# A two-layer cross-attention decoder on one core: earlier loads of rows and value weights, and later exponentials in one step

## Chip, core and metric

The kernel runs on one core of a Trainium2 chip. A core has five engines that run their own instruction queues: TensorE (PE in the profile; its weight loads are listed as PEld), VectorE (DVE), ScalarE (ACT), GpSimd (POOL) and SyncE (SP), which here only issues DMAs. ACT and POOL can issue DMAs too. The metric is the device time of one execution in microseconds (us). Before the change it is 2435.92 us, the median of three runs (2434.83 to 2436.45).

## The reference

Two batches of 512 rows of width 1024 (`x`) pass through four blocks, all in float32 unless noted. `ctx` has 1024 rows of width 1024 per batch.

```python
# layer 0
x = x + fake_quant(layernorm(x)) @ fake_quant(ctx)           # 8-bit grids: exact in bf16
x = x + h @ W.T + b + lora(h, softmax(mean(h) @ router))     # h = layernorm(x)
# layer 1
h = layernorm(x)
q = rope(h @ wq); k = rope(ctx @ wk); v = ctx @ wv           # 32 query heads, 8 key heads, width 128
a = softmax(q @ k.T / sqrt(128) + mask) @ v
x = x + a @ wo
x = x + layernorm(x) @ W_up.T + top-1 lora
```

Keys and values of layer 1 depend on `ctx` alone and not on `x`, so they can be computed first.

## The kernel before

**Seven products.** Every large float32 product is cut into 2 x 2 blocks and done with seven block products instead of eight (`seven`, L258, in the order 1, 2, 6, 7, 5, 4, 3; `seven_onto` for sums onto rows). Sums and differences of the operand blocks are made by VectorE: `left_steps` (L230; additions at L233, L236, L238, L241) for weights and `right_steps` (L244; L247, L250, L252, L255) for the context. A product accumulates in a PSUM bank; banks are shared by products 1 and 2, 7 and 4, 5 and 3. So product 2 must wait until ACT has copied product 1 out (L274), product 4 until VectorE has read product 7 (L281), and product 3 until VectorE has read product 5 (L283). Product 6 is read at L278, products 4 and 3 at L287 and L290. All of these matmuls go through `accumulate`, so their line is L345.

**Order of the stages.** TensorE's order is that of the program. The first stage is the keys of batch 0 (`keys`, L475): two quads of heads, each in two groups. Its loads stand at L1031 to L1070: key weights (pool `u4`, eight tiles of 4 KB per partition) and the four quarters of the transposed context (pool `u8`), on SP and ACT, then rope tables and small constants on SP. Each finished key block is turned by `rope` (L196; two ACT copies L204/L205, then VectorE L207, L210, L211) and stored by SP (L487). After the keys come the values of batch 0 (`values`), then keys and values of batch 1. Layer 0 (`layer_0`, `quantized_product`, L410) is woven between their products: for each batch eight row tiles of `ctx` are loaded (L414) and quantized by VectorE (L182, L185, L186), the four row tiles of `x` are normalized (`layernorm`: statistics L151 twice and L152 for each tile, square root on ACT L163, reciprocal L164, scaling L156) and quantized with the same three lines, then transposed (L424) and multiplied.

**What sets the order of the other engines.** A planner orders the instructions of each engine by when it expects their inputs, earlier lines of the program first. Inside `manual_schedule` blocks the named engines keep the program's order: VectorE and ACT in the first stage (L1088 to L1119), VectorE, ACT and POOL in the attention (L1287 on). Instructions from outside such a block may still be set between those of the block, where the planner expects a wait. Each pool has a fixed number of slots (`u8` 14, `u4` 17, `u2` 10, `small` 16). Slots are given in the program's order of first use, slots never used ahead of those given back; a tile's first writer waits for the slot's last user. SP and ACT issue DMAs in their own order, and an issue that waits holds up all behind it.

**The lines of this change.** The rows of batch 0 are loaded by `load_rows(0, nc.scalar)` (L1119), the last statement of the first stage's manual block, four DMAs of 512 KB on ACT. The first value weights are loaded by `raw_weights(wv, 0)` (L1144), four DMAs of 512 KB on SP, just before the second quad of keys is run and woven with layer 0; they are needed by the values' sums at L233 and following. 

**The attention's start.** `attention` (L851) runs one head per step n, from −2 on. In a step, the scores of head n+2 go to PSUM in four pairs (`scores`, L761; the two wide PSUM buffers), VectorE adds the mask and so frees each buffer (L777), and `tree` finds the maximum (L785 to L791), which is turned by TensorE into another wide buffer (L727) and reduced by VectorE (L729). For head n+1, `place_maximum` copies the maximum to a PSUM bank (L805) and `exponential` subtracts it (L809), takes the exponential on ACT (L812) and sums on POOL (L815 to L820). In steps −2 and −1 no head is ready for its products, and the last products of the queries fill TensorE instead: four of them in step −1 (L920), with the exponentials of head 0 set between them (L922 to L926). The ropes of these products are finished later, at `rotate` (L939).

Of the kernel before, what the change touches and what calls it, by code (L numbers as in the profile page):

```python
# [39 lines left out]
def decoder_kernel(  # L40
# [25 lines left out]
    nc = tc.nc  # L66
# [286 lines left out]

    def quad_weights(dram, q):

        return quad_sums(raw_weights(dram, q))

    def raw_weights(dram, q):
        raw = []
        for mh in range(2):  # L360
            for ch in range(2):
                w = u4([P, 4, 256])
                nc.sync.dma_start(w, dram[q, mh, ch])
                raw.append(w)
        return raw

    def quad_sums(raw):
        return left_sums(nc.vector, *raw, lambda: u4([P, 4, 256]))

    x = [None] * B  # L370
# [4 lines left out]
    def halves():  # L375
        return [u8([P, 2, D]) for _ in range(2)]
# [7 lines left out]
    def load_rows(b, queue):  # L384
        for t in range(NT):
            queue.dma_start(rows(b, t), x_in[b, ts(t, P), :])
# [464 lines left out]
    def attention(extra):  # L851

        total = B * NH
        heads, outs, kv = {}, {}, {}
        stretches = iter(())

        def rotate():  # L860
            for rotation in extra["later"]:
                next(rotation, None)
            extra["later"].clear()

        def begin(n):
            if n >= total:
                return
            gg = n // GRP
            if gg not in kv:
                b, g = gg // NKV, gg % NKV  # L870
                kT = u4([P, S2])
                nc.sync.dma_start(kT, kT_d[b][g])
                v = u4([P, NKT, DH])
                nc.sync.dma_start(v, v_d[b][g // 2][:, :, ts(g % 2, DH)])
                kv[gg] = kT, v
                outs[gg] = u8([P, GRP, S])
            heads[n] = Head(n, kv[gg], outs[gg][:, n % GRP, :])

        begin(0)
        for n in range(-2, total + GRP + 1):  # L880
            new, mid, old = heads.get(n + 2), heads.get(n + 1), heads.get(n)
            begin(n + 3)
            if new:
                for j in range(4):
                    new.scores(j)
            yield

            if n - 1 in heads:
                heads.pop(n - 1).normalize()
            if n == GRP - 1 or n == NH:  # L890
                fetch_rows(n // NH)

            if GRP <= n <= total and n % GRP == 0:
                oT = outs.pop(n // GRP - 1)
                sums = u8([P, 3, 2, 256])
                places = iter(range(3))
                o_ops = left_sums(
                    nc.gpsimd,
                    oT[:, 0:2, 0:256],
                    oT[:, 2:4, 0:256],  # L900
                    oT[:, 0:2, 256:S],
                    oT[:, 2:4, 256:S],
                    lambda: sums[:, next(places)],
                )
                following = n // GRP - 1, o_ops
            tree = new.tree() if new else iter(())
            k = (n - 1) % GRP
            if n > GRP and k == 0:
                gg, o_ops = following
                stretches = projection(gg // NKV, o_ops, dict(w_ops))  # L910
            for _ in range(3 + k % 2 if n > GRP else 0):
                next(stretches, None)
                next(tree, None)
            if n > GRP and gg + 1 < B * NKV:
                for i in {2: (1, 6, 2), 3: (7, 5, 4, 3)}.get(k, ()):
                    w_ops[i] = output_operand((gg + 1) % NKV, i)
            for i in range(extra.pop(n, 0)):
                for _ in range(2):
                    next(tree, None)
                next(extra["products"])  # L920

                if mid and not old and i == 1:  # L922
                    mid.place_maximum()
                    mid.exponential(0)
                if mid and not old and i == 2:
                    mid.exponential(1)  # L926
            if n == GRP:
                w_ops = {i: output_operand(0, i) for i in (1, 6, 2, 7, 5, 4, 3)}
            for _ in tree:
                pass  # L930
            yield

            if mid and old:
                mid.place_maximum()
            if old:
                old.turn_sum()
            elif new:
                new.turn_maximum()
            rotate()  # L939
            if old:  # L940
                old.attend(0)
                if mid:
                    mid.exponential(0)
                if new:
                    new.turn_maximum()
                if mid:
                    mid.exponential(1)
                old.den = from_row(old.den)
            if new:
                new.nmx = from_row(new.nmx)  # L950
            if old:
                old.attend(1)
            yield
# [114 lines left out]
    nc.sync.dma_start(eb_t, ebias.partition_broadcast(P))  # L1068
    nc.sync.dma_start(r0_t, r0T.rearrange("(c p) e -> p c e", p=P))
    nc.sync.dma_start(ga_t, gaT.rearrange("(c p) e -> p c e", p=P))  # L1070


    ctx_ops = [ctx_raw[0], ctx_raw[2]] + [None] * 5
    w = [wk_raw[q][0:2] + [None] * 5 for q in range(2)]
# [13 lines left out]
    with tc.manual_schedule(engines={mybir.EngineType.DVE, mybir.EngineType.Activation}):  # L1088
        rights = right_steps(nc.vector, *ctx_raw, lambda: u8([P, 4, HALF]))
        lefts = left_steps(nc.vector, *wk_raw[0], lambda: u4([P, 4, 256]))  # L1090
        advance(rights, 2)
        advance(lefts, 2)
        for c in range(4):
            for m in range(2):
                nc.tensor.matmul(
                    begun[m],
                    wk_raw[0][0][:, c, ts(m, P)],
                    ctx_raw[0][:, c, :],
                    start=(c == 0),
                    stop=(c == 3),  # L1100
                )
        for g in first[0]:
            next(g)
        next(first[0][0])
        next(rights)
        next(lefts)
        next(first[0][1])
        w[0][:] = next(lefts)
        ctx_ops[:] = next(rights)
        for _ in range(2):  # L1110
            for g in first[1]:
                next(g)
        lefts = left_steps(nc.vector, *wk_raw[1], lambda: u4([P, 4, 256]))
        for i, _ in enumerate(chain(*first[0])):
            if i in (4, 5, 6, 7):
                w[1][:] = next(lefts) or w[1]

        x[0] = halves()
        load_rows(0, nc.scalar)  # L1119

    for side in ("x1", "x2"):
        nc.vector.reciprocal(qp[f"{side}_inv"], qp[f"{side}_scale"])
    for c_t, side in ((c_x1, "x1"), (c_x2, "x2")):
# [5 lines left out]
    for b in range(B):  # L1129
        if b == 1:  # L1130
            for ch in range(2):
                ctx_raw[2 * ch + 1] = context_quarter(1, ch, 1, nc.scalar)
            w = quad_weights(wk, 0)
            ctx_ops = context_sums(ctx_raw)
        for i, stage in enumerate((keys, keys, values, values)):
            if (b, i) == (0, 0):
                continue
            if (b, i) == (0, 3):
                ctx_raw = [None] * 4
                for ch in range(2):  # L1140
                    ctx_raw[2 * ch] = context_quarter(1, ch, 0, nc.scalar)
            if (b, i) == (0, 1):
                main = chain(*first[1])
                raw = raw_weights(wv, 0)  # L1144
                weave(main, side, 2)
                w = quad_sums(raw)
            else:
                main = pair(*stage(b, i % 2, ctx_ops, w))
                weave(main, side, 2)
                if i < 3:  # L1150
                    w = quad_weights((wk, wv)[(i + 1) // 2], (i + 1) % 2)
            if i == 1 and b == 1:
                for _ in side:
                    pass
                ab_t = u8([P, 2, D])
                a_t, b_t = ab_t[:, 0].rearrange("p (c m) -> p c m", c=NC), ab_t[:, 1]
                nc.sync.dma_start(a_t, a0T.rearrange("(c p) m -> p c m", p=P))
                nc.gpsimd.dma_start(b_t, b0.partition_broadcast(P))  # L1158
                tT = [None] * B
                fetch_rows(0)  # L1160
                hs, steps = normed(0, u8, 2)
                side = chain(steps, routed(0, hs, a_t, b_t, tT))
# [30 lines left out]
    w = [quad_weights(wq, 0), quad_weights(wq, 1)]  # L1193
# [12 lines left out]
    for q in range(NH // 4):  # L1206
# [9 lines left out]
        if q < NH // 4 - 1:  # L1216
# [6 lines left out]
            if q > 0:  # L1223
                w = quad_weights(wq, q + 1)
# [207 lines left out]
```

## Time and profile before

| what | us |
|---|---|
| median of three runs | 2435.92 |
| profiled execution, whole | 2434.64 |
| its span, first to last instruction | 2432.8 |
| TensorE busy | 2407.8 |
| VectorE busy | 1842.8 |
| GpSimd busy | 1024.5 |
| ACT busy | 527.2 |
| rows of batch 0 issued (ACT, four) | 71.97 to 74.06 |
| value weights issued (SP, four) | 57.05 to 72.15 |
| last constant issued (SP) | 27.86 |

The profile is of one execution, so sums are made against 2434.64 and carried over to the median. A line of a timeline begins with the start and the duration in us; then come the engine, the line of the kernel, the operation, the tile written and the tiles read, their shapes and the number of merged instructions; the bracket holds the idle time just before and what ended it. In a table by stretches, the columns are the stretch's length, the busy time of TensorE, its weight loads, VectorE, ACT and POOL (with the number of instructions), the granted TensorE clock (1.00 is full), the busy share of the 16 DMA engines, and GB/s. TensorE's matmuls are pipelined, and their ends are modelled.

### The profile page before, as it was taken

How to read it: one execution, taken by the hardware profiler on the slowest of the kernel's cores; microseconds unless marked ns; L12 is line 12 of the kernel's file. 1: busy time of each engine (PE TensorE's matmuls, PEld its weight loads, DVE VectorE, ACT ScalarE, POOL GpSimd, SP SyncE). 2: the span in 40 equal slices, each digit the busy share in tenths (PEclk: the TensorE clock that was granted, in tenths of full speed). 3: DMA queues.
4: the chain of work that ended last, by engine and by line, in shares of the span. 5: the costliest groups of instructions: out<-in, count | busy, mean ns of one | idle time of the engine just before them, and what ended most of it. 6: DMA issues, size and time to landing. Idle time of an engine off the chain costs nothing.

```text
span 2432.8 us, 19529 instructions
## 1 busy us (share of the span) xinstructions
PE 2407.8 (99%) x6792; PEld 1195.1 (49%) x6792; DVE 1842.8 (76%) x1998; ACT 527.2 (22%) x623; POOL 1024.5 (42%) x543
## 2 busy tenths in 40 slices
PE   9999999999999999999999999999999999999999
PEld 4477458654444444444444444444444444444444
DVE  5849774345986556898888888888898988888753
ACT  1210221011222222322222222222223222222210
POOL 0000010210000002777676767667776767677531
PEclk9999999999999999999999999999999999999999
DMA  5437133013796221344223323442332243233501
GB/s 197 169 99 281 70 131 112 26 61 116 280 334 212 78 90 53 101 141 117 75 80 106 117 68 89 143 143 79 129 117 78 95 123 116 66 91 109 173 9 61
DMA packets 151506, 288.01 MB, mean 118 GB/s; under 512 B 32112, under 2 KB 49776, under 8 KB 149104
## 3 DMA queue, kind: packets, MB, share of 16 engines
q1 hardware_dynamic: 110880, 244.54, 30.6%
q10 hardware_dynamic: 40384, 41.70, 5.6%
q8 instruction: 54, 0.88, 0.1%
q0 software_dynamic: 144, 0.52, 0.1%
q14 instruction: 44, 0.36, 0.1%
HBM read 223.54 MB, written 63.18 MB: 118 GB/s over the span
## 4 chain that ended last, share of the span: by engine, by line
PE 55%; DVE 4%; issue 1%; POOL 0%; ACT 0%; POOLq 0%; DVEq 0%; ACTq 0%
PE b L345 20%; PE wide L763 16%; PE b L826 16%; PE wide L727 2%; DVE u L809 1%; DVE u L777 0%; DVE u L789 0%; DVE small L729 0%; DVE u L318 0%; DVE u L787 0%; PE b L967 0%; PE wide L192 0%; DVE u L791 0%; DVE u L785 0%; PE wide L1016 0%
## 5 line engine op out<-in xcount | busy, mean ns | idle before, releaser
L345 PE MATMUL b<-u,u 128*128 128x512 f32 (+1 forms) x3600 | 1384.5, 541 | 14.8 <-DVE u L283 4.2
L345 PEld LDWEIGHTS b<-u,u 128*128 128x128 f32 x3600 | 681.3, 191 | 684.0 <-issue 605.2
L826 PE MATMUL b<-u,u 128*128 128x512 f32 x1024 | 460.3, 592 | 0.0
L763 PE MATMUL wide<-u,u 128*128 128x512 f32 x1024 | 452.6, 593 | 2.6 <-DVE u L777 1.7
L815 POOL TENSOR_TENSOR u<-u 128x1024 f32<-128x1024 f32 x64 | 151.6, 2368 | 705.3 <-ACT u L812 696.8
L777 DVE TENSOR_TENSOR u<-wide,u 128x1024 f32<-128x1024 f32 x256 | 312.7, 1223 | 125.3 <-PE wide L763 125.1
L812 ACT ACTIVATE u<-u 128x2048 f32<-128x2048 f32 x128 | 244.7, 1911 | 665.1 <-DVE u L809 662.3
L763 PEld LDWEIGHTS wide<-u,u 128*128 128x128 f32 x1024 | 192.8, 190 | 250.9 <-issue 175.5
L809 DVE TENSOR_TENSOR u<-u,b 128x2048 f32<-128x2048 f32 x128 | 290.1, 2267 | 3.0 <-ACT b L805 3.0
L826 PEld LDWEIGHTS b<-u,u 128*128 128x128 f32 x1024 | 186.2, 192 | 184.6 <-issue 184.6
L300 POOL TENSOR_TENSOR u<-u,u 128x512 f32<-128x512 f32 x120 | 184.3, 1562 | 170.3 <-DVE u L312 134.6
L318 DVE TENSOR_TENSOR u<-u,b 128x512 f32<-128x512 f32 x200 | 135.6, 679 | 121.7 <-PE b L345 114.4
L818 POOL TENSOR_TENSOR u<-u,u 128x1024 f32<-128x1024 f32 x64 | 150.7, 2355 | 30.9 <-ACT u L812 30.7
L819 POOL TENSOR_TENSOR u<-u,u 128x1024 f32<-128x1024 f32 x64 | 150.8, 2356 | 5.0
L204 ACT ACTIVATE u<-u 64x512 f32<-64x512 f32 x72 | 45.2, 628 | 361.6 <-DVE u L283 162.5
L837 POOL TENSOR_TENSOR u<-u,u 128x512 f32<-128x512 f32 x64 | 115.0, 1797 | 18.4 <-DMA u<-row 18.4
L785 DVE TENSOR_TENSOR u<-u 128x1024 f32<-128x1024 f32 x64 | 113.0, 1765 | 0.0
L727 PEld LDWEIGHTS wide<-ident,u 128*128 128x128 f32 x512 | 79.9, 203 | 61.8 <-issue 55.7
L605 POOL TENSOR_TENSOR u<-u,u 128x1024 f32<-128x1024 f32 x8 | 20.2, 2528 | 213.0 <-DVE u L156 210.4
L787 DVE TENSOR_TENSOR u<-u,u 128x1024 f32<-128x1024 f32 x64 | 107.5, 1679 | 0.2
L820 POOL TENSOR_TENSOR u<-u 128x512 f32<-128x512 f32 x64 | 100.1, 1564 | 5.0
L1158 POOL DMA_DIRECT2D u<-in_b_dram x1 | 0.7, 717 | 229.1 <-PE b L345 229.1
(136 smaller groups left out, 1639.4 us busy)
## 6 DMA issues: line engine op xcount, KB each, us to landing
u<-row ACTq DMA_DIRECT2D x128, 256.0 KB, 3.5
u<-wo SPq DMA_DIRECT2D x64, 512.0 KB, 4.3
u<-in_wo_dram SPq DMA_DIRECT2D x48, 512.0 KB, 4.4
u<-in_wq_dram SPq DMA_DIRECT2D x32, 512.0 KB, 4.3
q<-u SPq DMA_DIRECT2D x64, 256.0 KB, 2.3
u<-in_wo_dram SPq DMA_DIRECT2D x16, 1024.0 KB, 8.0
wo<-u SPq DMA_DIRECT2D x32, 512.0 KB, 4.4
u<-q SPq DMA_DIRECT2D x64, 256.0 KB, 4.5
```

Source lines behind the costliest of these rows:

```text
L300: nc.gpsimd.tensor_tensor(c, c, what, ALU.add)
L318: nc.vector.tensor_tensor(c, c, acc, ALU.add)
L345: nc.tensor.matmul(acc, lhsT, rhs, start=start and k == 0, stop=k == len(pairs) - 1, skip_group_check=True,)
L727: nc.tensor.transpose(tr[:, t, :], src[:, t, :], ident)
L763: nc.tensor.matmul(sc[:, ts(n, HALF)], self.kT[:, ts(2 * j + n, P)], self.qT, start=True, stop=True,)
L777: nc.vector.tensor_tensor(self.e[j // 2][:, js, :], sc.rearrange("p (k q) -> p k q", k=2), mask[j], ALU.add)
L809: nc.vector.tensor_tensor(e, e, self.nmf.unsqueeze(1).to_broadcast([P, 4, S]), ALU.add)
L812: nc.scalar.activation(e, e, AF.Exp)
L815: nc.gpsimd.tensor_tensor(d, e[:, 0:2, :], e[:, 2:4, :], ALU.add)
L818: nc.gpsimd.tensor_tensor(d, d, e[:, 0:2, :], ALU.add)
L819: nc.gpsimd.tensor_tensor(d, d, e[:, 2:4, :], ALU.add)
L826: nc.tensor.matmul(self.acc, self.v[:, k, :], self.e[j][:, k % 4, :], start=(k == 0), stop=(k == NKT - 1),)
```

## The change

Three edits. The four loads of batch 0's rows move from the end of the first stage, on ACT, to just behind the small constants, on SP. The four loads of the first value weights move from SP to POOL; their place in the program stays. In step −1 of the attention, the two exponentials of head 0 come after the third and fourth product instead of after the second and third; `place_maximum` stays after the second.

```diff
     def quad_weights(dram, q):
-        return quad_sums(raw_weights(dram, q))
+        return quad_sums(raw_weights(dram, q, nc.sync))

-    def raw_weights(dram, q):
+    def raw_weights(dram, q, queue):
         raw = []
         for mh in range(2):
             for ch in range(2):
                 w = u4([P, 4, 256])
-                nc.sync.dma_start(w, dram[q, mh, ch])
+                queue.dma_start(w, dram[q, mh, ch])
                 raw.append(w)
         return raw
...
                 if mid and not old and i == 1:
                     mid.place_maximum()
-                    mid.exponential(0)
-                if mid and not old and i == 2:
-                    mid.exponential(1)
+                if mid and not old and i > 1:
+                    mid.exponential(i - 2)
...
     nc.sync.dma_start(ga_t, gaT.rearrange("(c p) e -> p c e", p=P))
+    x[0] = halves()
+    load_rows(0, nc.sync)
...
-        x[0] = halves()
-        load_rows(0, nc.scalar)
...
             if (b, i) == (0, 1):
                 main = chain(*first[1])
-                raw = raw_weights(wv, 0)
+                raw = raw_weights(wv, 0, nc.gpsimd)
                 weave(main, side, 2)
                 w = quad_sums(raw)
```

## The prediction

> **What bounds the kernel now.** I read the page first, then TensorE's timeline with the waits in brackets, then VectorE's timeline ahead of each wait, then the table by stretches.
>
> ```profile
> PE 2407.8 (99%) x6792; PEld 1195.1 (49%) x6792; DVE 1842.8 (76%) x1998; ACT 527.2 (22%) x623; POOL 1024.5 (42%) x543
> ```
>
> TensorE is idle for 2432.8 − 2407.8 = 25.0 us in all, so a change that adds no matmul can win little, and each new idle microsecond on TensorE is a microsecond of the end. The order of TensorE's instructions is the program's and is not touched. Nearly half of the idle time lies ahead of 126 us:
>
> ```profile
> 44.60 38.03 PE L345 MATMUL b<-u,u 128*128 128x512 f32 x88 [0.49 <-DVE u L281]
> 86.09 15.70 PE L345 MATMUL b<-u,u 128*128 128x512 f32 x32 [3.45 <-DVE u L283]
> 102.80 3.70 PE L345 MATMUL b<-u,u 128*128 128x512 f32 x8 [1.02 <-DVE u L281]
> 107.25 14.06 PE L345 MATMUL b<-u,u 128*128 128x512 f32 x56 [0.75 <-DVE u L283]
> ...
> 125.88 9.69 PE L345 MATMUL b<-u,u 128*128 128x256 f32 x32 [4.11 <-ACT u L274]
> 135.85 7.12 PE L345 MATMUL b<-u,u 128*128 128x256 f32 x32
> ```
>
> The four waits from 86 us sum to 3.45 + 1.02 + 0.75 + 4.11 = 9.3. The long two cost more: 32 matmuls that take 7.12 at 135.85 take 9.69 at 125.88 (+2.6), and at 86.09 the granted clock is down (column before last but one, 0.70; here 9 matmuls in 5 us where the stretch before has 13: +1.7). Together 9.3 + 4.3 = 13.6 us. VectorE shows why:
>
> ```profile
> 23.96 2.29 DVE L250 TENSOR_TENSOR u<-u,u 128x2048 f32<-128x2048 f32 x1 [1.67 <-DMA u<-in_ctxT_in_dram]
> ...
> 43.86 0.69 DVE L281 TENSOR_TENSOR u<-u,b 128x512 f32<-128x512 f32 x1
> ...
> 77.41 0.69 DVE L151 BATCH_NORM_STATS2 small<-u 128x6 f32<-128x512 f32 x1 [2.13 <-DMA u<-in_x_in_dram]
> ...
> 79.99 0.81 DVE L182 TENSOR_SCALAR u<-u,qp_x_inv,qp_x_zp 128x1024 f32<-128x1024 f32 x1 [1.31 <-DMA u<-in_ctx_in_dram]
> ...
> 84.63 0.81 DVE L182 TENSOR_SCALAR u<-u,qp_x_inv,qp_x_zp 128x1024 f32<-128x1024 f32 x1 [1.90 <-DMA u<-in_ctx_in_dram]
> 85.35 0.68 DVE L283 TENSOR_TENSOR u<-u,b 128x512 f32<-128x512 f32 x1
> ```
>
> From L250 to L281 it works back to back for 19.9 us and TensorE waits for the end of that. In 77 to 85 it waits 2.13 + 1.31 + 1.90 = 5.3 for transfers, with L283 queued behind the last; from 84.6 to 136.5 it is busy almost throughout. The transfers, by stretches (us, then busy time of each engine, clock, DMA share, GB/s):
>
> ```profile
> 10.00:20.00 10.00, 10.00 (x25) 4.33 (x24) 0.00 (x0) 2.35 (x4) 0.00 (x0) 1.00 1.04 398
> 30.00:40.00 10.00, 10.00 (x24) 4.37 (x23) 10.00 (x14) 2.36 (x4) 0.00 (x0) 1.00 0.15 54
> 77.00:82.00 5.00, 5.00 (x13) 2.17 (x12) 3.29 (x6) 0.00 (x0) 0.00 (x0) 1.00 1.02 396
> 87.00:92.00 5.00, 5.00 (x9) 1.98 (x8) 5.00 (x9) 0.39 (x1) 0.00 (x0) 0.70 0.76 293
> ```
>
> DMA is full to 26 us and again around 80, and nearly idle between.
>
> **Value weights to GpSimd's queue: +2.6 us at the start.** Four issues leave SP (57.05 to 71.77) and go ahead of GpSimd's only other early one (b0's, 230.56), which they don't reach. Pool u4 gives its 17 slots in program order, unused ones first. Ahead of these tiles stand eight key weights, one table tile and 3 + 3 sums: 15. So the first two value weights find unused slots, and on a queue with nothing ahead (GpSimd's last instruction begins at 1.18) they start at about 2 us: 2 × 0.524 MB amid the first stage's loads. Two readings: a queue of its own is free (0), or it shares. The Trainium skill (DMA: Bandwidth & Descriptors, "Issuing engines are not separate DMA queues") says that all queues run on the same 16 engines and interleave, and another issuer saves only issue time. With the row at 398 GB/s full, I take the rule: 1.05 MB / 0.398 = 2.6 us later for the context quarter of L250. Part may show earlier, as a wait in the first products; the total is the same. The other two wait for slots that L238 (33.9) and L241 (37.0) release, move at a DMA share of 0.15, and are needed at 115. The skill (SBUF — State Buffer, "SBUF: two separate sides", the "DVE blocks DMA" trap) says that GpSimd cannot write descriptors while VectorE is in a two-port mode, which speaks against this queue; the one row, b0's load beside a busy VectorE, lands in 4.3 us like SP's. With 75 us of cover either gives 0.
>
> **Rows behind the constants: +4.3, and a clock loss of 1.7.** Four issues leave ACT (72 to 74, behind the last rope) and follow the constants on SP at about 28 + 2.6, some 0.4 us each, so 1.6 us ahead of the first key store (30.60). Their 2.1 MB take 5.3 us; the first stores land that much later. Their source slots in u2 are wanted near L281; cover about 10 us, price if it is gone at most 5. The square root's table load (1.28, now at 82.19) comes earlier on ACT, which is idle more than half of that time: 0. The rows then lie in SBUF by 38 instead of 77 to 82, and the planner, which puts ready instructions without a fixed place into waits that it foresees on VectorE (the reciprocals L1122 sit inside two ropes, at 29.77 and 35.03), will put statistics there. Row 3's come behind a later `small` tile, so rows 0 to 2: six L151 at 0.61, three L152 at 0.13, three L164 at 0.08 = 4.3 us. L278 ran at 43.08 though its product ended near 37.2: the planner saw gaps where the chip, late since the start, has none. So before L281 they add between 0 and 4.3; I take 4.3. L281 goes to 43.86 + 2.6 + 4.3 = 50.8, TensorE's restart from 44.60 to 51.5. The product before ends near 46 to 47, so it idles 4 to 5 us and I add the clock loss of the nearest row, 3.45 idle: 1.7 (upper end 2.6, of 4.11 idle). Early cost 2.6 + 4.3 + 1.7 = 8.6, low end 2.6.
>
> **What both give back: −10.2.** The stretch 66 to 87 loses 2.1 MB of rows and the value weights, so the context rows land sooner: VectorE's 5.3 of transfer waits go, and 4.3 of statistics are already done: 9.6 us of VectorE time against 9.3 of TensorE waits. The 3.45 goes with the transfer ahead of L283. The 4.11 is ACT's copy L274 (125.24), queued behind a square root (L163, 124.81) that waited for statistics (124.57): gone too. But the planner makes a new order, in a stretch where VectorE stays nearly full. I take three quarters of 13.6 = 10.2; ends 4.5 (a third) and 13.6.
>
> **Exponentials a product later: +1.7.** VectorE's timeline in this step:
>
> ```profile
> 955.05 2.29 DVE L809 TENSOR_TENSOR u<-u,b 128x2048 f32<-128x2048 f32 x1 [2.98 <-ACT b L805]
> 957.26 0.68 DVE L278 TENSOR_TENSOR u<-u,b 128x512 f32<-128x512 f32 x1
> 957.85 2.28 DVE L809 TENSOR_TENSOR u<-u,b 128x2048 f32<-128x2048 f32 x1
> 961.73 0.69 DVE L281 TENSOR_TENSOR u<-u,b 128x512 f32<-128x512 f32 x1 [1.60 <-PE b L345]
> 962.34 0.68 DVE L729 TENSOR_REDUCE small<-wide 128x4 f32<-128x512 f32 x1
> ```
>
> TensorE's wait of 1.25 at 957.99 is for L278, behind the first L809. Moved ahead of it, L278 starts when its product ends, 956.78: 0.5 won. But the second L809 now stands behind L281: L281 at 961.25, L809 at 961.86, L729 at 964.07 instead of 962.34. L729 frees the wide buffer of the next head's second score pair, which could start at 963.24 and starts at 964.8; the third waits for L777 (two L207 later), 967.1 against 965.44 now. From there TensorE is 1.7 later. GpSimd's sums move by 2 to 4, covered by its waits at 976 and 980. Ends: −0.5 and +2.2.
>
> **Sum.** +8.6 − 10.2 + 1.7 = +0.1 on the profiled execution of 2434.64 (span 2432.8 and 1.8 around it). The median shown is 1.3 above it: 2435.92 + 0.1, about 2436.0.
>
> **Rivals.** *Faster:* the planner sets the statistics behind L281, into ACT waits of 1.3 us at 46 to 56, and all late waits go: 2.6 − 13.6 + 1.7 = −9.3, 2426.6. For it: those gaps exist. Against: they come second. *Slower:* VectorE remains the bound from 84 to 136. Place: its queue at L281/L283 of the key stage; price: only a third returns, 8.6 − 4.5 + 1.7 = +5.8, 2441.7; it decides once less than 5.4 of the 13.6 comes back. For it: no VectorE work is removed and the keys' stage has few gaps. *The early loads aren't early* (GpSimd's loads start with the slot order, near 66): no 2.6 and no clock loss, −4.2, 2431.7, inside the forecast's band.
>
> **How the numbers follow.** 0.2% is 4.9 us, about what a measurement can tell here. Forecast 0.36 and the not-early case 0.08, both within 0.2%: 0.44. Slower: 0.30, since the early costs have one sign and the return rests on an order not yet known. Faster: 0.26, since one guess about that order carries 6 us. The range reaches from the faster case (2427) to a high end of 8.6 + 0.9 + 1.7 − 1 = +10, 2446; the forecast's own range is 2431 to 2441.
>
> **What would show it.** Right: GpSimd issues at about 2 us; L250 near 26.6; L151 ahead of L281 and a TensorE wait of some 4 us near 50 with the clock down; waits from 86 on summing under 3; L729 in the step of 957 about 1.7 later against L278. Wrong: context quarter on time, L281 within 3 us of 43.86, or a wait over 3 us after 80.

## The result, and the profile after

The changed kernel takes 2447.01 us in the median of six runs (2443.24 to 2449.98). The kernel before, on the same chip, takes 2436.18. The ratio is 1.0041, with a 95% interval of 1.0031 to 1.0051: slower by about 10 us, and 1 us above the predicted range. The span of the profiled execution is 2444.9 us instead of 2432.8. Line numbers from the attention on differ by one or two in the new kernel: L1096 is L1095 of before, and L1120 to L1124 are L1122 to L1126. The kernels of the experiments are shifted likewise (L1121 and L365 there are L1122 and L363).

TensorE's timeline in the first 140 us:

```profile
11.78 3.67 PE L1096 MATMUL b<-u,u 128*128 128x512 f32 x8 [2.66 <-DMA u<-in_ctxT_in_dram]
15.28 13.98 PE L345 MATMUL b<-u,u 128*128 128x512 f32 x32
44.95 73.86 PE L345 MATMUL b<-u,u 128*128 128x512 f32 x168 [15.68 <-ACT u L274]
119.38 14.06 PE L345 MATMUL b<-u,u 128*128 128x512 f32 x56 [0.57 <-DVE u L283]
135.47 4.80 PE L345 MATMUL b<-u,u 128*128 128x256 f32 x21 [1.59 <-ACT u L274]
```

The late waits are nearly gone, as forecast: 0.57 and 1.59 stand where before had 3.45, 1.02, 0.75 and 4.11. But there is one wait of 15.68 us that the prediction did not have at all. It is for ACT's copy of product 1. The table by stretches (columns as in the table of before) shows TensorE without a matmul for two whole stretches, and what the wait does to the clock:

```profile
32.00:38.00 6.00, 0.00 (x0) 0.00 (x0) 4.27 (x3) 0.00 (x0) 0.00 (x0) 0.69 0.98 341
38.00:44.00 6.00, 0.00 (x0) 0.00 (x0) 6.00 (x9) 1.17 (x1) 0.00 (x0) 0.50 0.08 31
44.00:50.00 6.00, 5.05 (x9) 2.30 (x10) 6.00 (x8) 1.37 (x4) 0.53 (x1) 0.67 0.36 120
```

The granted clock falls to 0.50 during the wait and stays there behind it: stretches of 1 us show 0.50 or 0.51 from 44 to 48 us and 1.00 from 48 us on. VectorE's and ACT's timelines show what is late:

```profile
30.90 0.16 DVE L1120 RECIPROCAL qp_x_inv<-qp_x_scale 128x1 f32<-128x1 f32 x1 [28.97 <-DMA qp_x_scale<-in_x_scale_dram]
...
31.67 2.28 DVE L247 TENSOR_TENSOR u<-u,u 128x2048 f32<-128x2048 f32 x1
35.68 0.69 DVE L151 BATCH_NORM_STATS2 small<-u 128x6 f32<-128x512 f32 x1 [1.73 <-DMA u<-in_x_in_dram]
36.29 2.27 DVE L250 TENSOR_TENSOR u<-u,u 128x2048 f32<-128x2048 f32 x1
...
60.47 0.69 DVE L281 TENSOR_TENSOR u<-u,b 128x512 f32<-128x512 f32 x1 [1.54 <-PE b L345]
```
```profile
42.83 1.28 ACT L163 ACT_TABLE_LOAD   x1 [19.20 <-DVE small L152]
44.13 0.29 ACT L163 ACTIVATE small<-small,eps_one 128x1 f32<-128x1 f32 x1
44.33 1.05 ACT L274 COPY u<-b 128x512 f32<-128x512 f32 x2
```

The lines of before at the same places:

```profile
20.00 2.29 DVE L247 TENSOR_TENSOR u<-u,u 128x2048 f32<-128x2048 f32 x1 [18.07 <-DMA u<-in_ctxT_in_dram]
```
```profile
23.55 0.58 ACT L274 COPY u<-b 128x512 f32<-128x512 f32 x1 [2.24 <-PE b L345]
26.98 0.58 ACT L274 COPY u<-b 128x512 f32<-128x512 f32 x1 [2.85 <-PE b L345]
```

The first context sum L247 begins at 31.67. Before, it began as soon as its quarter of the context landed, at 20.00. Now six small operations on the constants (L1120 to L1124) stand ahead of it on VectorE, and the constants are the last thing that SP loads ahead of the rows. The second sum L250 stands behind a statistic of the rows (L151), at 36.29 instead of 23.96. On ACT the square root L163, which waits for the statistics, stands ahead of the two copies L274, which before ran at 23.55 and 26.98. GpSimd's timeline has the early loads as predicted:

```profile
1.61 1.25 POOL L363 DMA_DIRECT2D u<-in_wv_dram  x2
47.23 0.53 POOL L363 DMA_DIRECT2D u<-in_wv_dram  x1 [44.37 <-DVE u L238]
```

So the time can be followed at equal points of TensorE's work. At the group of 56 matmuls the new kernel is 119.38 − 107.25 = 12.1 us behind. There before has already paid 3.45 + 1.02 + 0.75 of waits and 1.7 of clock; without those, and without the new kernel's 0.57, the early part cost 12.13 + 6.92 − 0.57 = 18.5 us, where the prediction had 8.6. At 344 us the lag is 7.2, at the first scores (924) 8.9, and 11.6 behind the first attention steps (1053).

### The profile page after: what moved, and what is told of

It reads as the page before. It is cut to its first block, busy times and chain, and to the rows that moved or that the text cites. A ratio compares the mean times of both kernels' runs of the same rounds, so it can differ in the third digit from the quotient of the medians.

```text
span 2444.9 us, 19529 instructions
## 1 busy us (share of the span) xinstructions
PE 2404.6 (98%) x6784; PEld 1193.2 (49%) x6792; DVE 1842.5 (75%) x1998; ACT 527.2 (22%) x623; POOL 1027.9 (42%) x547
## 4 chain that ended last, share of the span: by engine, by line
PE 85%; DVE 7%; issue 2%; POOL 1%; DMA 1%; ACT 1%; SPq 0%; POOLq 0%; DVEq 0%; ACTq 0%
PE b L345 48%; PE wide L763 16%; PE b L826 15%; PE wide L727 2%; DVE u L809 2%; PE wide L461 1%; PE wide L192 1%; DMA u<-in_wo_dram 1%; PE b L651 1%; DVE small L729 0%; DVE u L789 0%; DVE u L777 0%; DVE u L787 0%; DVE u L318 0%; DVE u L210 0%
## 5 line engine op out<-in xcount | busy, mean ns | idle before, releaser
L777 DVE TENSOR_TENSOR u<-wide,u 128x1024 f32<-128x1024 f32 x256 | 312.7, 1224 | 125.0 <-PE wide L763 124.8
L809 DVE TENSOR_TENSOR u<-u,b 128x2048 f32<-128x2048 f32 x128 | 290.3, 2268 | 0.0
L787 DVE TENSOR_TENSOR u<-u,u 128x1024 f32<-128x1024 f32 x64 | 107.6, 1681 | 0.2
L789 DVE TENSOR_TENSOR u<-u,u 128x1024 f32<-128x1024 f32 x64 | 95.5, 1492 | 0.1
```

Source lines behind the costliest of these rows:

```text
L777: nc.vector.tensor_tensor(self.e[j // 2][:, js, :], sc.rearrange("p (k q) -> p k q", k=2), mask[j], ALU.add)
L809: nc.vector.tensor_tensor(e, e, self.nmf.unsqueeze(1).to_broadcast([P, 4, S]), ALU.add)
```

## The experiments

The theory after this reading is "sums behind the rows". Slots of pool u8 are given in the program's order of first use. In the changed program the rows' tiles come ahead of the context sums, so the sums get their slots behind the rows' loads. The planner, which then takes the sums to be ready only behind the rows' loads, places the small constants' operations and the first statistics ahead of them. On the chip no sum lacks a slot (four context quarters, two row tiles and three sums take 9 of u8's 14), and L247 has no wait in its bracket: it is late through its place in VectorE's order alone. What the planner reckons is in no trace; the runs below can show only what the order of first use does. The rivals are contention (the early value weights delay everything), the early statistics as such (the prediction's own step), and the square root on ACT.

| kernel | ratio to before (95%) | profiled span | start of the 56 matmuls | start of the 64 matmuls near 344 us |
|---|---|---|---|---|
| before | | 2432.8 | 107.25 | 343.76 |
| the change | 1.0041 (1.0031 to 1.0051) | 2444.9 | 119.38 | 350.95 |
| rows alone | 1.0036 (1.0023 to 1.0048) | 2442.4 | 120.86 | 352.68 |
| value weights alone | 1.0008 (1.0000 to 1.0017) | 2434.8 | 106.08 | 344.55 |
| exponentials alone | 1.0013 (1.0007 to 1.0020) | 2436.0 | 107.02 | 342.83 |
| rows, sums' slots first | 0.9993 (0.9985 to 1.0001) | 2435.5 | 109.96 | 341.40 |
| the change, sums' slots first | 0.9999 (0.9991 to 1.0007) | 2434.5 | 107.51 | 339.16 |
| rows, no square root | 1.0025 (1.0017 to 1.0032) | 2436.3 | 115.87 | 347.41 |
| rows on ACT, earlier | 0.9966 (0.9954 to 0.9979) | 2429.0 | | 334.98 |
| and weights on GpSimd, late | 0.9986 (0.9977 to 0.9994) | 2432.7 | | 339.10 |
| and weights on GpSimd, in the gap | 0.9963 (0.9951 to 0.9976) | 2426.3 | 101.48 | 333.03 |
| rows on ACT, exponentials between | 0.9967 (0.9955 to 0.9979) | 2430.4 | 103.88 | 335.28 |

(No number: TensorE's groups are cut elsewhere in that timeline. TensorE's own order is the program's, and the same in all of them. The ratio is of medians, the span of one execution; for the exponentials alone and the rows without the square root that one is the fastest of all.)

**Rows alone.** The kernel before with only this edit:

```diff
     nc.sync.dma_start(ga_t, gaT.rearrange("(c p) e -> p c e", p=P))
+    x[0] = halves()
+    load_rows(0, nc.sync)
...
-        x[0] = halves()
-        load_rows(0, nc.scalar)
```

> Only the rows' loads move (behind the constants, on SP); value weights and exponentials as before. Theory 'sums behind the rows' (u8 slots are given in program order, so the context sums L247 and L250 get theirs only behind the rows' loads, and are placed behind the small constants' operations): L247 still starts some 8 us late (28 to 29 against 20.00), the square root still stands ahead of ACT's copies, and most of the early cost of 18.5 us stays, about 16; total about 2442.5. Rival 'contention' (the early value weights are what delays the first stage): L247 within 1 us of 20.00, and with the return kept the total is under 2436. Rival 'statistics' (the prediction's own step): L247 and L250 on time, L281 some 4 us late, total near 2434.

Slower by 0.36%, most of the whole change. TensorE and VectorE:

```profile
42.28 71.51 PE L345 MATMUL b<-u,u 128*128 128x512 f32 x160 [14.43 <-ACT u L274]
```
```profile
27.99 0.16 DVE L1121 RECIPROCAL qp_x_inv<-qp_x_scale 128x1 f32<-128x1 f32 x1 [26.06 <-DMA qp_x_scale<-in_x_scale_dram]
...
28.77 2.28 DVE L247 TENSOR_TENSOR u<-u,u 128x2048 f32<-128x2048 f32 x1
```

L247 is 8.8 us late with no value weight loaded early, and the long wait is there with 14.43 us. Contention is ruled out as the cause of the long wait. It adds about 3 us to the start: L247 of the whole change is 2.9 later still.

**Value weights alone.**

```diff
-                nc.sync.dma_start(w, dram[q, mh, ch])
+                queue.dma_start(w, dram[q, mh, ch])
...
-                raw = raw_weights(wv, 0)
+                raw = raw_weights(wv, 0, nc.gpsimd)
```

> Only the value weights move to GpSimd's queue. Theory 'sums behind the rows': two of the four loads start at about 2 us and the context quarter of L250 lands 2.6 us later, L250 near 26.6, L281 near 46.5; some of the late waits go, since SP's queue is shorter; total 2435 to 2438.5. Rival 'contention': most of the early cost of 18.5 us is here, total 2446 or more.

```profile
22.94 2.29 DVE L247 TENSOR_TENSOR u<-u,u 128x2048 f32<-128x2048 f32 x1 [21.01 <-DMA u<-in_ctxT_in_dram]
26.90 2.29 DVE L250 TENSOR_TENSOR u<-u,u 128x2048 f32<-128x2048 f32 x1 [1.67 <-DMA u<-in_ctxT_in_dram]
```

L250 begins at 26.90 against 23.96 (+2.9), and TensorE's restart behind L281 moves from 44.60 to 47.54 (+2.9). At the 56 matmuls the kernel is 1.2 us ahead of before, since SP's shorter queue brought the context rows earlier. A wait of 6.00 us for ACT's copy at 126.59, where before had 4.11, takes that back. The ratio touches 1.

**Exponentials alone.**

```diff
                     mid.place_maximum()
-                    mid.exponential(0)
-                if mid and not old and i == 2:
-                    mid.exponential(1)
+                if mid and not old and i > 1:
+                    mid.exponential(i - 2)
```

> Only the two exponentials move one product later. The prediction's step holds: 0.5 won at L278, 1.7 lost at L729 and its wide buffer; the offset of TensorE grows by 1.7 to 1.8 within the step, total about 2437.9. Rival 'later waits take it' (the step's end is set by something else): total within 0.5 us of before.

TensorE's timeline in the step:

```profile
958.25 3.70 PE L345 MATMUL b<-u,u 128*128 128x512 f32 x8 [0.85 <-DVE u L278]
962.26 1.88 PE L763 MATMUL wide<-u,u 128*128 128x512 f32 x4
965.53 1.98 PE L763 MATMUL wide<-u,u 128*128 128x512 f32 x4 [1.39 <-DVE small L729]
967.86 3.70 PE L763 MATMUL wide<-u,u 128*128 128x512 f32 x8 [0.34 <-DVE u L777]
971.40 7.03 PE L345 MATMUL b<-u,u 128*128 128x512 f32 x16
...
990.34 3.70 PE L763 MATMUL wide<-u,u 128*128 128x512 f32 x8 [0.67 <-DVE u L777]
```

The wait for L278 shrinks from 1.25 to 0.85, and new waits of 1.39 for L729 and 0.34 for L777 come in. Against the first scores (924.46 before, 925.12 here) the next products start 971.40 − 968.94 − 0.66 = 1.8 us later, as predicted. The next step adds a wait of 0.67 for L777, and at the products behind it the lag in the attention is 1015.42 − 1012.02 − 0.66 = 2.7 us. The timed runs say 0.13%, some 3 us.

**Rows, with the sums' slots first.** The rows' loads stay where the change puts them. The three context sums take their slots ahead of them:

```diff
+    sums_r = [u8([P, 4, HALF]) for _ in range(3)]
+    for t in sums_r:
+        nc.gpsimd.memset(t[:, 0, 0:1], 0.0)
     x[0] = halves()
     load_rows(0, nc.sync)
...
-        rights = right_steps(nc.vector, *ctx_raw, lambda: u8([P, 4, HALF]))
+        rights = right_steps(nc.vector, *ctx_raw, lambda: sums_r.pop(0))
```

> As the rows alone, with the rows' loads at the same place in SP's queue, but the three context sums take their u8 slots first (a one-element memset on GpSimd each, ahead of the rows in the program). Theory 'sums behind the rows': L247 back at about 20.0, L250 at about 24.0, both L274 copies of the second quad ahead of the square roots; what remains is the prediction's step, statistics ahead of L281, some 4 us, against a return of 8 to 11: total 2431 to 2435. Rivals 'statistics' and 'SP's queue' (rows in VectorE's and SP's early order are enough): total within 2 us of the rows alone.

```profile
19.91 2.29 DVE L247 TENSOR_TENSOR u<-u,u 128x2048 f32<-128x2048 f32 x1 [17.99 <-DMA u<-in_ctxT_in_dram]
23.93 2.29 DVE L250 TENSOR_TENSOR u<-u,u 128x2048 f32<-128x2048 f32 x1 [1.72 <-DMA u<-in_ctxT_in_dram]
...
48.07 0.69 DVE L281 TENSOR_TENSOR u<-u,b 128x512 f32<-128x512 f32 x1
```

```profile
48.86 53.43 PE L345 MATMUL b<-u,u 128*128 128x512 f32 x120 [3.25 <-issue]
```

L247 and L250 are back to 19.91 and 23.93, with the rows at the same place of SP's queue. SP's position and the early rows as such are ruled out as the cause of the late sums and of the long wait. L281 is at 48.07 instead of 43.86, and TensorE restarts at 48.86 (L281 ends at 48.76; the bracket names no releaser) instead of 44.60: +4.3 us, six statistics and what belongs to them, the very step that the prediction had costed. The time is that of before within its interval (0.9985 to 1.0001).

**The whole change, with the sums' slots first.** The same edit, in the changed kernel.

> The whole change, with the three context sums given their u8 slots ahead of the rows (one-element memsets on GpSimd). Theory 'sums behind the rows': this is the schedule that the prediction assumed: L247 near 22.9 and L250 near 26.9 (2.9 us late, as measured for the weights alone), statistics ahead of L281, TensorE's restart near 51.5, no wait of TensorE over 6 us; total 2436 to 2441, 6 to 11 us under the change as made. Rival 'each early load costs by itself' (SP's queue, statistics on VectorE, shared transfers): total 2444 or more.

```profile
22.82 2.29 DVE L247 TENSOR_TENSOR u<-u,u 128x2048 f32<-128x2048 f32 x1 [20.89 <-DMA u<-in_ctxT_in_dram]
26.82 2.29 DVE L250 TENSOR_TENSOR u<-u,u 128x2048 f32<-128x2048 f32 x1 [1.71 <-DMA u<-in_ctxT_in_dram]
...
50.97 0.69 DVE L281 TENSOR_TENSOR u<-u,b 128x512 f32<-128x512 f32 x1
```
```profile
51.76 55.17 PE L345 MATMUL b<-u,u 128*128 128x512 f32 x128 [1.55 <-issue]
107.51 14.06 PE L345 MATMUL b<-u,u 128*128 128x512 f32 x56 [0.58 <-DVE u L283]
```

The prediction had L281 at 50.8 and the restart at 51.5; here they are at 50.97 and 51.76. It had 2436.0 us; this kernel takes 2436.31, beside 2435.97 for before on the same chip. Three memsets of one element are worth the 10 us that the change loses. That the total agrees to 0.3 us is in part luck. At 344 us this kernel is 343.76 − 339.16 = 4.6 us ahead of before, where the prediction's terms make 10.2 − 8.6 = 1.6. The stage of the queries, which the prediction left out, takes 3.9 of them (754.71 against 755.38 behind it), and the exponentials 2.7 instead of 1.7.

**Rows, without the square root.** The rows alone, but the row norm divides by the variance and not by its root, so its numbers are other ones and ACT has nothing to do for it:

```diff
-        nc.scalar.activation(rstd, mv[:, 1:2], AF.Sqrt, bias=eps_t)
+        nc.vector.tensor_scalar(rstd, mv[:, 1:2], EPS, None, ALU.add)
         nc.vector.reciprocal(rstd, rstd)
```

> The rows alone, with the square root left out of the row norm (the rows are scaled by the reciprocal of the variance, two small operations on VectorE), so that ACT has nothing between the two products' copies. Theory 'sums behind the rows': VectorE starts L247 at the same late time (28 to 29) and is what TensorE waits for in the end; the wait of 14.4 us for ACT's copy goes, and waits for VectorE's L278 or L281 of 10 us or more stand in its place; total within 3 us of the rows alone. Rival 'square root' (ACT's order alone makes the stall): no TensorE wait over 5 us before 80 us, total 2437 or less.

```profile
39.25 8.97 PE L345 MATMUL b<-u,u 128*128 128x512 f32 x16 [5.25 <-DVE u L207]
52.65 56.90 PE L345 MATMUL b<-u,u 128*128 128x512 f32 x128 [4.43 <-DVE u L207]
```

L247 is still at 28.72. The one long wait is replaced by two of 5.25 and 4.43, for VectorE's L207; I had expected 10 us or more at L278 or L281. At the 56 matmuls the lag is 115.87 − 107.25 = 8.6 us, against 13.6 for the rows alone. So of the 13.6, 5.0 go when the square root no longer stands ahead of ACT's copies, and 8.6 stay, with VectorE's late start and the statistics. The timed runs are 0.11% apart, under 3 us, and their intervals overlap: there the part of the square root is not shown.

**Rows on ACT, earlier.** Value weights and exponentials as before; the rows' loads move up within ACT's order:

```diff
         for i, _ in enumerate(chain(*first[0])):
             if i in (4, 5, 6, 7):
                 w[1][:] = next(lefts) or w[1]
+            if i == 3:
+                x[0] = halves()
+                load_rows(0, nc.scalar)
...
-        x[0] = halves()
-        load_rows(0, nc.scalar)
```

> The rows' four loads stay on ACT but stand behind the seventh product of the first two heads (some 50 us into the kernel instead of 72), value weights and exponentials as before. Theory 'the return is real, the place is wrong': up to 48 us nothing differs from before (L247 at 20.0, L281 at 43.9), statistics fall into VectorE's gaps between 58 and 80, the late waits of 9.3 us fall under 4 and total 2425 to 2430. Rival 'VectorE stays the bound from 84 to 136': the waits only move, total within 2 us of before.

```profile
44.57 51.79 PE L345 MATMUL b<-u,u 128*128 128x512 f32 x120 [0.71 <-DVE u L281]
98.41 19.19 PE L345 MATMUL b<-u,u 128*128 128x512 f32 x64 [2.04 <-DVE u L281]
119.64 7.17 PE L345 MATMUL b<-u,u 128*128 128x256 f32 x32 [1.59 <-ACT u L274]
```

The loads are issued at 49.31 to 51.12, the restart stays at 44.57, six of the statistics L151 run between 53 and 67, and the waits from 80 us on are 2.04 and 1.59 instead of 9.3. At 344 us the kernel is 8.8 us ahead, and the time is 2429.3 against 2435.97: 0.34% faster (0.21% to 0.46%). The return that the prediction saw is real, and it can be had without the early cost.

**The same, with the value weights on GpSimd.** First held back to the end of the stage by a one-element memset on VectorE:

```diff
+            if i == 8:
+                wv_raw = [u4([P, 4, 256]) for _ in range(4)]
+                for t in wv_raw[:2]:
+                    nc.vector.memset(t[:, 0, 0:1], 0.0)
...
-                raw = raw_weights(wv, 0)
+                raw = raw_weights(wv, 0, nc.gpsimd, wv_raw)
```

> As the last one, and the value weights on GpSimd's queue, held back until the end of the first stage by a one-element memset on VectorE for each of the first two. Theory 'the return is real, the place is wrong': no transfer is added to the first 25 us, SP's queue is free for the context rows, total 1 to 4 us under the last one, 2422 to 2428. Rival 'GpSimd's queue itself costs' (its issues, or descriptors held up by VectorE): total 2 us or more above the last one, and value weights landing late.

This missed: 0.9986, and a median 3.4 us above that of the last kernel (2432.74 against 2429.3; the two intervals just touch). Three of the four loads were issued from 72.79 on, just ahead of the context rows (77.46), and VectorE's first context row came late:

```profile
83.44 0.81 DVE L182 TENSOR_SCALAR u<-u,qp_x_inv,qp_x_zp 128x1024 f32<-128x1024 f32 x1 [1.51 <-DMA u<-in_ctx_in_dram]
```

Without the weights' move that row began at 77.87. TensorE then waited 5.11 us for L281 at 101.91. But SP also issued its first context row later, behind one more key store. Its line without the weights' move, and with it:

```profile
73.46 0.41 SPq L414 DMA_DIRECT2D u<-in_ctx_in_dram  x1
```
```profile
77.46 4.13 SPq L414 DMA_DIRECT2D u<-in_ctx_in_dram  x6
```

Of the 5.6 us by which L182 is late, 4.0 are this later issue; at most 1.6 are left for transfers that share the DMA engines. Whether GpSimd's queue itself was at fault is told by the next kernel, in which the first two tiles wait for the last context sum instead:

```diff
+                if after is not None and len(raw) < 2:
+                    nc.gpsimd.tensor_copy(w[:, 0, 0:1], after[:, 0, 0:1])
                 queue.dma_start(w, dram[q, mh, ch])
...
-                raw = raw_weights(wv, 0)
+                raw = raw_weights(wv, 0, nc.gpsimd, ctx_ops[3])
```

> Rows on ACT behind the seventh product of the first two heads, and the value weights on GpSimd's queue behind a one-element copy of the last context sum into the first two tiles, so that they start some 10 us earlier than in the last kernel (about 60 us instead of 73) and lie ahead of the context rows instead of among them. Theory 'it is the time of the transfers, not the queue': context rows no longer wait behind value weights, L182 starts at 78 or earlier, total within 2 us of the kernel with the rows on ACT alone (2429), or 1 to 3 us under it. Rival 'GpSimd's queue itself costs': total 3 us or more above it, as in the last kernel.

```profile
40.01 2.29 POOL L365 DMA_DIRECT2D u<-in_wv_dram  x4 [0.38 <-issue]
```
```profile
75.73 0.81 DVE L182 TENSOR_SCALAR u<-u,qp_x_inv,qp_x_zp 128x1024 f32<-128x1024 f32 x1
```

They were issued at 40.01, earlier than the 60 I had expected. The stretch from 32 to 50 us had a DMA share of 0.12 to 0.19 before. L182 begins at 75.73 and waits for nothing. The time is 2428.1, 0.37% under before (0.24% to 0.49%): the fastest kernel of the study by its median, though its interval and that of the rows on ACT alone overlap nearly whole. SP issued its first context row at 67.88 here. So GpSimd's queue by itself costs nothing that these runs can show. But they don't show that the time of the transfers decides: the moment at which SP issues the first context row (73.46, 77.46 and 67.88 in the three kernels) moved with it.

**Rows on ACT, with both exponentials after the third product.**

```diff
                     mid.place_maximum()
-                    mid.exponential(0)
                 if mid and not old and i == 2:
+                    mid.exponential(0)
                     mid.exponential(1)
```

> Rows on ACT behind the seventh product, value weights as before, and in step -1 of the attention both exponentials after the third product, ahead of L281 but behind L278. The prediction's account of this step (L278 gains 0.5 by standing ahead of the first L809; L729 loses only if an L809 stands behind L281): TensorE 0.4 to 0.6 earlier behind this step, no wait for L729, total 0.5 under the kernel with the rows alone (2428.8). Rival 'any later exponential is late': 1 us or more above it.

This missed too. VectorE runs L278 at 953.50, then both L809 to 958.59, L281 at 958.50 and L729 at 959.10, and TensorE does not wait for L729. From the first scores to the last product of the step it is 954.25 − 921.11 = 33.14 us against 954.03 − 920.49 = 33.54: 0.4 won. But waits of 0.31 and 0.21 for L777 take it back, and one step later, 987.73 − 921.11 = 66.62 stands against 986.52 − 920.49 = 66.03: 0.6 lost. By TensorE's timelines the order of before is the best of the three; the timed runs don't tell it from this one (0.9966 and 0.9967).

## Why the prediction was wrong

**The step that failed** is "Rows behind the constants: +4.3". The prediction let the statistics be set behind the context sums and ahead of L281, and left the sums themselves where they were. It took the rows as an addition to a fixed order. In the kernel as made they changed the order: L247 went behind the constants (+8.8 us in the rows alone), and the square root went ahead of ACT's copies of product 1. That step measured 13.6 us at the 56 matmuls for the rows alone, return already counted; with the sums' slots claimed first it is 2.7 at the same place, and 4.3 at the restart (48.86 against 44.60), as the prediction had it. A second term of the step failed with it: the square root on ACT, put at 0 because ACT is idle more than half of that time. ACT was idle, but its copies L274 stood behind the waiting square root until 44.33 in the kernel as made, and with the rows alone 5.0 of the 13.6 go without the square root. For pool u4 the prediction counted free slots. The same count for u8 (9 of 14) shows no wait either; what it left out is that the order of first use, in which the rows' tiles now come ahead of the sums', also sets the planner's order.

**Value weights, +2.6 at the start:** held, 2.9 measured, on L250 and on the restart alike. The reading that a queue of its own is free would have been wrong: GpSimd's two loads delayed SP's and ACT's, as the section of the Trainium skill that the prediction weighed (DMA: Bandwidth & Descriptors, "Issuing engines are not separate DMA queues") has it. The trap by which a busy VectorE would hold up GpSimd's issues did not show: at 40.01 four of them took 2.29 us beside a VectorE without a gap, and at 1.61 two took 1.25. No run here shows whether VectorE was in a two-port mode at 40.01.

**Clock, +1.7:** held, in kind and nearly in size. In the kernel as made the wait is 15.68, but behind it the clock is at 0.50 for only the first 3.05 us of matmuls (44.95 to 48), which makes some 1.5 us, my estimate from that clock. The length of the wait is counted in the step of the rows.

**Return, −10.2 of 13.6:** held. The late waits fell from 9.3 to 2.2, and both clock losses at 86 and 126 went: 7.1 + 4.3 = 11.4. So the "slower" rival, in which VectorE stays the bound and only a third returns, ended on the right side for a wrong reason.

**Exponentials, +1.7:** held within the step at 1.8, and undersized: the next step adds 0.9 through L777, 2.7 in all.

**The sum.** +18.5 early, −11.4 late, +2.7 in the attention make +9.8. The span is 12.1 longer. Of the remaining 2.3, 1.8 lie between 344 and 764 us: TensorE waits 0.78, 0.85 and 0.93 for VectorE at 635 to 764, where before had 0.40 and 0.33. The exponentials alone, whose VectorE order is that of before up to the attention, show the same waits (0.98, 0.85, 0.48), so they need not come from the early loads. The last 0.5 is not traced.

## What to carry to other kernels

Where slots and places in an order are given out by the program's order of first use, a load that is moved up takes a place in that order too: look for every tile whose first use it now precedes, in each pool, before costing the transfer itself. Move early loads into a gap that the table by stretches shows, and behind the tiles that the critical engine needs next; here that was worth 0.34%, and the same loads on SP, ahead of the context sums, cost 0.36%. A queue of its own gave no bandwidth: the value weights on GpSimd's queue cost 2.9 us of start at 2 us and nothing to be seen at 40 us; at 73 us the kernel lost 3.4 us, along with a later issue of the context rows on SP.

## What was not expected

The stage of the queries, from 600 to 765 us, moves by several microseconds from kernel to kernel without being touched. Its VectorE waits for output and query weights (before, L247 at 623.94 waits 0.56 us for one; with the exponentials alone, in the same order, 2.86), at a DMA share of 0.59 from 600 to 640 us and 0.91 and 0.98 in the two stretches of 40 us behind it. The kernels that come to it early keep only part of their lead: with the rows on ACT it is 8.8 us at 344 us and 755.38 − 751.43 = 4.0 us at 755; with the rows and the sums' slots first, a lead of 2.4 turns into a lag of 2.5. The value weights alone and the rows alone, which come late, lose 0.6 and 0.7 there, the change itself 1.8. That the transfers of this stage are its limit would fit this, but no run here was made to show it.
